# A two-block attention and feed-forward kernel: the start, the row maxima, the gated unit and the drawn order are changed

## The chip, the cores and the metric

The kernel runs on one core of one Trainium2 chip. The metric is the device time of one execution in microseconds (us); the median of three runs is 1132.83.

## The reference

The input x has 128 sequences of 64 tokens with 128 features (8192 tokens), and so has a context c. Four blocks follow each other, each with a residual addition:

```python
x = x + L0_xattn(layernorm(x), ctx)   # normalises again, 16 heads of 8, sigmoid gate, normalises its output
x = x + L0_ffn(layernorm(x))          # silu(x W1) * (x W2), two 512x512 layers with gelu, 512 to 128
x = x + L1_xattn(layernorm(x), ctx)   # 16 heads of 8, softmax, output projection
x = x + L1_ffn(layernorm(x))          # relu(x W1 + b1) W2 + b2
```

Everything is in 32-bit floats. The softmax subtracts a maximum per row before the exponential.

## The kernel before

The 8192 tokens are cut into 17 chunks: the first and the last have two groups of 128 tokens, the other fifteen have four. Each chunk passes through the four blocks (`attention0`, `ffn0`, `attention1`, `ffn1`). Each block is written as a Python generator that yields one operation (`Op`) at a time with the engine, a name, the buffers that it takes (`get`) and gives back (`put`). A planner (`Order`) runs on the host while the program is built. At each step it takes, among the operations that are next in their streams, the one that can start first by a table of durations (`LENGTHS`), and issues its instructions. So the order on every engine is fixed by the planner. It keeps a clock for each engine. Where two operations could start at the same time, priority decides, plus a small pseudo-random number (`draw`) whose seed comes from the list `DRAWS`, one entry for each 50 us of the planner's TensorE clock; a seed of 0 means that nothing is added.

```python
seed = DRAWS[min(int(self.clock[PE] / STRETCH), len(DRAWS) - 1)]
...
key = (t + (0.6 if other else 0.0), prio + s.op.draw, n)
```

TensorE (PE) writes to eight banks of PSUM. A score tile takes four banks of one half at once; all else takes one. In the first 95 us of the planner's clock, `fill` puts matmuls of zeros into gaps that the planner sees on PE:

```python
n = int((t - self.clock[PE]) * 0.8 / FILLER)   # FILLER is 0.11
```

Before that, `busy(60, 7)` issues sixty such matmuls (L428) by hand at the very start. Their operand is filled by GpSimd (POOL), and nothing reads what they write.

The loads go out from SyncE's queue at the start, in an order written by hand: the first chunk's context and input, the small constants, the first attention's weights (`wa`), the second chunk, and then the larger weights and the third chunk. `landed` holds when the planner takes each of them to be there; its clock begins with the first landing, which is about 3 us after the start of the trace.

The start of a chunk runs through these lines. VectorE (DVE) takes the moments (L541, L543), POOL makes a reciprocal square root (L526 to L559), ScalarE (ACT) or DVE normalises (L568, L572), PE transposes (L582), ACT or DVE scales and copies (L589, L591), and PE multiplies for keys (L618), queries (L606) and values (L631). ACT or DVE writes masked copies of keys and queries (L597, L599), for which the masks (L479 to L487) must be there.

Attention works on half a chunk at a time (`attend`): scores (L658, packed in rows of the array), the row maxima from PSUM (L662, DVE), the maxima as three bf16 parts (L672 to L675, DVE or POOL), their transposition (L679) and copy (L682, ACT), the scores once more with the maxima taken off (L691, with the selection matrix `asel`), the exponential (L696, ACT), the weighted values (L710, packed in columns, with the value buffer `vblk`), masking (L720 to L724), reciprocal (L727, L728) and the product on POOL (L742). The operation for the maxima takes one of four buffers `nm` and gives back all four banks when it is over.

The value buffers `vblk` (three) and the buffers `nm` (four) are filled with constants by POOL at the start (`blanks`: L493, L496, L498), each as soon as POOL is free for it. The additions of a row vector to x (L848, L1070, L1092) are POOL's too, and so are the sums of weights that the multiplication scheme of the two 512x512 layers needs (L896).

The gated unit (`gated`, four times a chunk) takes two banks at once, issues both products (L903, L904), then tanh (L907, ACT) and two fused operations on DVE (L909, L910) as one operation. Its result goes into the two square layers (`square`): differences on POOL (L938), products (L956), sums (L982) and gelu (L975).

Of the kernel before, what the change touches and what calls it, by code (L numbers as in the profile page):

```python
# [18 lines left out]
SEQ = 64  # L19
# [7 lines left out]
HS = 4  # L27
# [11 lines left out]
for _n, _w in _COLS:  # L39
# [10 lines left out]
N_VB, N_NM = 3, 4  # L50
# [11 lines left out]


STRETCH = 50.0
DRAWS = [97, 0, 427, 0, 249, 0, 0, 0, 575, 0, 0, 112, 0, 817, 0, 39, 412, 0, 615, 329, 0, 15, 762, 0]
SPREAD = 0.1
SWAP = [*range(16, 32), *range(16)]

# [2 lines left out]
PE, DVE, ACT, POOL, SP = "PE", "DVE", "ACT", "POOL", "SP"  # L71
NONE = ""
# [4 lines left out]
    PE: {  # L77
        "bias": (0.22, 0.25), "transpose": (0.46, 0.15), "q": (0.86, -0.2), "k": (0.94, -0.2), "v": (0.89, 0.15),
        "scores": (0.99, 0.2), "max transpose": (0.07, 0.2), "scores less max": (1.17, 0.2),
        "weighted values": (0.92, 0.2), "tokens": (0.22, 0.15), "tokens 4": (0.9, 0.15), "w12": (1.73, -0.2),  # L80
        "product": (0.865, -0.2), "f1": (0.865, -0.2),
    },
    DVE: {
        "bias+": 0.28, "masks": 1.2, "gate weights": 0.4, "folds": 1.9, "moments": 1.07, "z": 1.3, "copied": 0.68,
        "scaled": 0.75, "qx": 1.5, "kx": 1.5, "vb": 1.8, "max": 2.3, "parts": 0.8, "reciprocal": 2.2, "o2": 0.83,
        "from bank": 0.68, "gate sums": 1.3, "gate": 0.4, "gained": 1.1, "gated": 1.45, "sum": 0.68, "saved": 0.68,
        "relu": 0.7,
    },
    ACT: {
# [233 lines left out]
def kernel(  # L323
# [16 lines left out]
    nc = tc.nc  # L340
# [65 lines left out]
    order = Order(RESOURCES)  # L406
# [3 lines left out]
    hm = load("hm", [P, 2, 2, 2], headmask.rearrange("p (n s t) -> p n s t", n=2, s=2))  # L410
# [15 lines left out]
    def busy(n, bank):  # L426
        for _ in range(n):
            nc.tensor.matmul(banks[:, bank, 0:P], blank, blank, start=True, stop=True)  # L428

    order.busy = busy  # L430
    busy(60, 7)
    ident = const.tile([P, P], F32, tag="ident", name="ident")
    make_identity(nc, ident)

    mask = const.tile([P, 4], F32, tag="mask", name="mask")
    half_mask = const.tile([P, 2, 4], F32, tag="half_mask", name="half_mask")
# [39 lines left out]

    def masks():
        yield Op(DVE, "masks")
        nc.vector.tensor_tensor(half_mask[:, 0, 0:2], hm[:, 0, 0, :], hm[:, 0, 1, :], ALU.add)  # L479
        nc.vector.tensor_tensor(half_mask[:, 1, 0:2], hm[:, 1, 0, :], hm[:, 1, 1, :], ALU.add)  # L480
        nc.vector.tensor_tensor(half_mask[:, 0, 2:4], hm[:, 0, :, 0], hm[:, 0, :, 1], ALU.add)
        nc.vector.tensor_tensor(half_mask[:, 1, 2:4], hm[:, 1, :, 0], hm[:, 1, :, 1], ALU.add)
        nc.vector.tensor_tensor(mask, half_mask[:, 0, :], half_mask[:, 1, :], ALU.add)
        for t, i, name in (
            (bk0, 2, "L0_xattn_bk"), (bq0, 0, "L0_xattn_bq"), (bk1, 2, "L1_xattn_b_k"), (bq1, 0, "L1_xattn_b_q"),
        ):
            nc.vector.tensor_scalar(t, mask[:, i : i + 2], colv(name), None, ALU.mult)  # L487

    def blanks():

        for i in range(N_NM):
            yield Op(POOL, "blank", put=[("nm", i)])
            nc.gpsimd.memset(nmax[i], 0.0)  # L493
            if i < N_VB:
                yield Op(POOL, "blank values", put=[("vb", i)])
                nc.gpsimd.memset(vblk[i], 0.0)  # L496
                for par in range(2):
                    nc.gpsimd.memset(vblk[i][64 * par : 64 * par + 64, :, 1, par, :], 1.0)  # L498
# [4 lines left out]
    fold = const.tile([P, 2, 32], F32, tag="fold", name="fold")  # L503
# [139 lines left out]
    def attend(got, half, halves):  # L643
# [11 lines left out]
        for s in range(HS):  # L655
            for g in range(4):
                h = slice(32 * g, 32 * g + 32)
                nc.tensor.matmul(sc[:, g, s, :], qs[h, s, :], ks[h, s, :], start=True, stop=True)  # L658
        mx = yield Op(DVE, "max", get={"nm": 1}, put=pe.slots["sc"])
        nm = nmax[mx.slots["nm"][0][1]]  # L660
        m = small.tile([P, 4, 2 * HS], F32, tag="m", name="m")
        nc.vector.tensor_reduce(  # L662
            m,
            sc.rearrange("p g s (j k) -> p g (s j) k", j=2),
            AX.X,
            ALU.max,
            negate=True,
        )
# [125 lines left out]
    def folds():  # L794

        yield Op(DVE, "folds")

        nc.vector.tensor_copy(identb, ident)
        nc.vector.tensor_tensor(
            fold, ident[:, 0:64].rearrange("p (r c) -> p r c", r=2), ident[:, 64:128].rearrange("p (r c) -> p r c", r=2), ALU.add  # L800
        )
        nc.vector.tensor_tensor(fold[:, 0, :], fold[:, 0, :], fold[:, 1, :], ALU.add)
        for j in range(1, 3):
            nc.vector.tensor_tensor(
                fold[:, 0, 0:8], fold[:, 0, 0:8], fold[:, 0, 8 * j : 8 * j + 8], ALU.add
            )
        for s in range(HS):
            nc.vector.tensor_copy(
                asel[:, s, :].rearrange("p (j k) -> p j k", j=2),
                fold[:, 0, 2 * s : 2 * s + 2].unsqueeze(2).to_broadcast([P, 2, 64]),  # L810
            )
# [86 lines left out]
        made_weights[l] = [a[0][0], a[0][1], s[2], a[1][1], s[0], s[1], a[1][0]]  # L898

    def gated(k, zT, n, free, d):  # L900
        pe = yield Op(PE, "w12", get={"bank": 2, "wk": 1}, put=free)
        pa, pb = (tile_of(s, (P, n)) for s in pe.slots["bank"])
        nc.tensor.matmul(pa, w12[:, 0, k * P : (k + 1) * P], zT, start=True, stop=True)  # L903
        nc.tensor.matmul(pb, w12[:, 1, k * P : (k + 1) * P], zT, start=True, stop=True)  # L904
        yield Op(ACT, "tanh", prio=-1)
        th = tile_of(pe.slots["wk"][0], (P, n))
        nc.scalar.activation(th, pa, AF.Tanh, scale=half_s1[:, k : k + 1])  # L907
        yield Op(DVE, "gated", put=pe.slots["bank"] + pe.slots["wk"], prio=-1)
        nc.vector.scalar_tensor_tensor(th, th, 1.0, pa, ALU.add, ALU.mult)  # L909
        nc.vector.scalar_tensor_tensor(  # L910
            d[k // 2][0][:, :, k % 2, :],
            th.rearrange("p (t c) -> p t c", t=2),
            half_s12[:, k : k + 1],
            pb.rearrange("p (t c) -> p t c", t=2),
            ALU.mult,
            ALU.mult,
        )
# [97 lines left out]
    def ffn0(ci, prio):  # L1015
        xt, ng = x_sb[ci], GROUPS[ci]
        z, fz = yield from normalised(xt, ng)
        zT, fz = yield from transposed(z, ng, fz)
        fz = Last(fz, 4)
        b, made = {}, []  # L1020
        n = ng * P
        yield from two_halves(b, n)
# [174 lines left out]
```

## Time and profile before

| | us |
|---|---|
| median of three runs (lowest, highest) | 1132.83 (1132.09, 1133.68) |
| the profiled execution, whole | 1132.17 |
| its span, first to last instruction | 1130.3 |
| PE busy | 1100.1 |
| DVE busy | 866.8 |
| ACT busy | 726.0 |
| POOL busy | 504.9 |

The profile is of one execution. A row of a group gives the line, the engine, the operation, what is written and read, how often, the busy time and the mean duration of one. PE's busy time counts matmuls whose ends are modelled; PEld is the loading of weights, which overlaps them. The granted clock is the share of its full clock that PE was given.

### The profile page before, as it was taken

What the parts mean: (1) busy time and instruction counts of PE and PEld (TensorE: products, weight loads), DVE (VectorE), ACT (ScalarE), POOL (GpSimd) and SP (SyncE); (2) the same over time, 40 slices, a digit from 0 to 9 for tenths busy, and PEclk for the clock granted to TensorE, in tenths of its full rate; (3) what the DMA queues carried; (4) which work ended last, traced back from release to release, by engine and by line L of the source; (5) the groups of instructions that cost most, each with busy time, mean ns of one, the idle gap of its engine ahead of it and who ended that gap; (6) DMA issues with size and microseconds to landing.
All of it is one profiled execution on the core that took longest, in us unless ns stands there. A gap on an engine that the chain in (4) does not pass through costs nothing.

```text
span 1130.3 us, 32935 instructions
## 1 busy us (share of the span) xinstructions
PE 1100.1 (97%) x13871; PEld 868.5 (77%) x13871; DVE 866.8 (77%) x2139; ACT 726.0 (64%) x1279; POOL 504.9 (45%) x882
## 2 busy tenths in 40 slices
PE   7699999999999999999999999999999999999998
PEld 6577687778876778878676887777778887789786
DVE  7887969889877777567978687788789888643773
ACT  5467767666775776576646686667867675545553
POOL 6745545445534445333326355335345546352221
PEclk9999999999999999999999999999999999999999
DMA  7001000000001001001100000000000000000001
GB/s 244 12 2 29 21 11 21 11 1 20 12 2 34 2 2 39 1 3 38 49 20 20 11 21 11 12 19 12 11 11 12 11 7 11 1 1 1 12 20 43
DMA packets 35444, 23.23 MB, mean 21 GB/s; under 512 B 1504, under 2 KB 34272, under 8 KB 35168
## 3 DMA queue, kind: packets, MB, share of 16 engines
q1 hardware_dynamic: 35296, 21.13, 6.3%
q8 instruction: 109, 1.79, 0.7%
q14 instruction: 39, 0.32, 0.1%
HBM read 16.93 MB, written 4.19 MB: 19 GB/s over the span
## 4 chain that ended last, share of the span: by engine, by line
PE 87%; DVE 9%; ACT 2%; issue 1%; POOL 1%; DVEq 0%; ACTq 0%; POOLq 0%
PE banks L956 33%; PE banks L770 12%; PE banks L691 7%; PE banks L710 5%; PE banks L658 5%; PE banks L1080 5%; PE banks L903 4%; PE banks L904 4%; PE banks L582 4%; DVE m L662 3%; PE banks L631 3%; PE banks L618 2%; PE banks L606 2%; DVE su L727 1%; PE banks L428 1%
## 5 line engine op out<-in xcount | busy, mean ns | idle before, releaser
L662 DVE TENSOR_REDUCE m<-banks 128x32 f32<-128x2048 f32 x64 | 145.9, 2281 | 17.6 <-PE banks L658 16.9
L742 POOL TENSOR_TENSOR wk<-av,rec 128x256 f32<-128x256 f32 x64 | 46.9, 733 | 220.6 <-DVE rec L728 198.0
L696 ACT ACTIVATE e<-banks 128x2048 f32<-128x2048 f32 x64 | 120.2, 1877 | 36.3 <-PE banks L691 29.1
L956 PE MATMUL banks<-hd,wh 128*128 128x256 f32 (+1 forms) x544 | 127.7, 371 | 0.4 <-DVE wk L909 0.4
L956 PE MATMUL banks<-wk,wh 128*128 128x256 f32 (+1 forms) x544 | 127.5, 371 | 0.0
L956 PE MATMUL banks<-wk,ws 128*128 128x256 f32 (+1 forms) x544 | 126.3, 371 | 0.8 <-POOL wk L938 0.7
L727 DVE RECIPROCAL su<-su 128x256 f32<-128x256 f32 x64 | 111.5, 1742 | 0.0
L956 PEld LDWEIGHTS banks<-wk,wh 128*128 128x128 f32 x544 | 96.4, 190 | 18.0 <-issue 5.7
L975 ACT ACTIVATE hd<-hd,col 128x256 f32<-128x256 f32 (+1 forms) x204 | 88.8, 488 | 31.7 <-DVE hd L982 30.9
L956 PEld LDWEIGHTS banks<-hd,wh 128*128 128x128 f32 x544 | 95.4, 190 | 16.4 <-issue 4.1
L956 PEld LDWEIGHTS banks<-wk,ws 128*128 128x128 f32 x544 | 94.7, 190 | 16.5 <-issue 3.3
L982 DVE TENSOR_TENSOR hd<-banks,hd 128x512 f32<-128x512 f32 (+1 forms) x102 | 66.7, 656 | 52.9 <-PE banks L956 45.3
L529 POOL TENSOR_TENSOR nr<-nv,neg_half 128x4 f32<-128x4 f32 (+1 forms) x102 | 99.7, 978 | 8.5
L938 POOL TENSOR_TENSOR wk<-hd,wk 128x512 f32<-128x512 f32 (+1 forms) x68 | 82.4, 1212 | 40.4 <-DVE hd L910 29.0
L512 ACT COPY hd<-banks 128x512 f32<-128x512 f32 (+1 forms) x68 | 37.9, 557 | 73.0 <-PE banks L956 67.9
L568 ACT ACTIVATE wk<-x,nb,nr 128x128 f32<-128x128 f32 x192 | 79.0, 484 | 7.1 <-POOL nb L559 6.8
L658 PEld LDWEIGHTS banks<-kx,qx 32*128 32x128 f32 x2048 | 62.8, 186 | 22.4 <-issue 10.0
L710 PEld LDWEIGHTS banks<-e,vblk 128*32 128x32 f32 x4096 | 60.2, 110 | 24.0 <-issue 7.6
L658 PE MATMUL banks<-kx,qx 32*128 32x128 f32 x2048 | 74.6, 282 | 2.5 <-ACT qx L597 1.2
L710 PE MATMUL banks<-e,vblk 128*32 128x64 f32 x4096 | 70.4, 220 | 2.2 <-ACT e L696 2.2
L691 PE MATMUL banks<-qx,kx 32*128 32x128 f32 x2048 | 71.7, 277 | 0.0
L909 DVE SCALAR_TENSOR_TENSOR wk<-wk,banks 128x512 f32<-128x512 f32 (+1 forms) x68 | 43.9, 646 | 33.1 <-ACT wk L907 33.0
(136 smaller groups left out, 2399.2 us busy)
## 6 DMA issues: line engine op xcount, KB each, us to landing
c<-in_c_dram SPq DMA_DIRECT2D x30, 256.0 KB, 3.0
x<-in_x_dram SPq DMA_DIRECT2D x15, 256.0 KB, 3.6
out_dram<-x SPq DMA_DIRECT2D x15, 256.0 KB, 2.3
wh<-in_w_h_dram SPq DMA_DIRECT2D x1, 2048.0 KB, 12.4
c<-in_c_dram SPq DMA_DIRECT2D x4, 128.0 KB, 2.7
wa<-in_w_a_dram SPq DMA_DIRECT2D x2, 256.0 KB, 5.1
w<-in_w_dram SPq DMA_DIRECT2D x1, 512.0 KB, 7.9
wf<-in_w_f_dram SPq DMA_DIRECT2D x2, 256.0 KB, 6.7
```

Of the source, the lines that this page charges most:

```text
L529: nc.gpsimd.tensor_tensor(rs, ve, neg_half[:, 0:ng], ALU.pow)
L568: nc.scalar.activation(z[:, g, :], src[:, g, :], AF.Identity, bias=nb[:, g : g + 1], scale=rs[:, g : g + 1])
L658: nc.tensor.matmul(sc[:, g, s, :], qs[h, s, :], ks[h, s, :], start=True, stop=True)
L662: nc.vector.tensor_reduce(m, sc.rearrange("p g s (j k) -> p g (s j) k", j=2), AX.X, ALU.max, negate=True,)
L691: nc.tensor.matmul(sT[:, g, s, :], lhs, rhs, start=(n == 0 and s == 0), stop=(n == 1), skip_group_check=True)
L696: nc.scalar.activation(e.rearrange("p g s i q -> p (g s i q)"), sT.rearrange("p g s c -> p (g s c)"), AF.Exp, scale=SCALE,)
L710: nc.tensor.matmul(po[32 * g : 32 * g + 32, i, s, :], vb[:, 4 * (half * HS + s) + g, i : i + 2].rearrange("p h j d -> p (h j d)"), e[:, g, ...
L727: nc.vector.reciprocal(su, su)
L770: nc.tensor.matmul(ps[:, g, :], lhs(g), w, start=(n == 0), stop=(n == len(blocks) - 1),)
L938: nc.gpsimd.tensor_tensor(T[m][0], x(), y(), ALU.subtract)
L956: nc.tensor.matmul(pieces[bank][0][:, o], w[:, k, o * P : (o + 1) * P], x[:, k], start=(new and k == 0 and o == 0), stop=(k == 1), skip_gr ...
L975: nc.scalar.activation(out(i, t)[:, o], (src or out(i, t))[:, o], AF.Gelu, scale=colv(scale, 2 * i + o))
```

## The change

Six things are changed. Forty zero-matmuls are issued at the start instead of sixty, and the planner's PE clock is set to 2.5 us behind them. The masks are made by two reductions over two axes instead of five additions, and the fold and the selection matrix by one reduction and one copy instead of four additions and four copies. The third value buffer's fill, and the fourth small one behind it, wait until the planner's clock has passed the landing of the first square layer's weights (24 us). The row maxima are taken in two operations of two banks each; the first gives back two banks, and only the second takes the buffer `nm`. The gated unit's second product is a stream of its own with priority 2, taking its own bank; the fused DVE operations become two planner operations. The durations in the planner's table follow these, and `DRAWS` is a new list without zeros.

```diff
-DRAWS = [97, 0, 427, 0, 249, 0, 0, 0, 575, 0, 0, 112, 0, 817, 0, 39, 412, 0, 615, 329, 0, 15, 762, 0]
+DRAWS = [71454, 18189, 18189, 18189, 18189, 68446, 18189, 18189, 18189, 18189, 35898, 18189, 18189, 18189, 23663, 18189, 18189, 18189, 39503, 18189, 49075, 18189, 62786, 18189]
...
-    busy(60, 7)
+    busy(40, 7)
+    order.clock[PE] = 2.5
...
-        nc.vector.tensor_tensor(half_mask[:, 0, 0:2], hm[:, 0, 0, :], hm[:, 0, 1, :], ALU.add)
-        nc.vector.tensor_tensor(half_mask[:, 1, 0:2], hm[:, 1, 0, :], hm[:, 1, 1, :], ALU.add)
-        nc.vector.tensor_tensor(half_mask[:, 0, 2:4], hm[:, 0, :, 0], hm[:, 0, :, 1], ALU.add)
-        nc.vector.tensor_tensor(half_mask[:, 1, 2:4], hm[:, 1, :, 0], hm[:, 1, :, 1], ALU.add)
-        nc.vector.tensor_tensor(mask, half_mask[:, 0, :], half_mask[:, 1, :], ALU.add)
+        for i, order_of in ((0, "p n s t -> p t n s"), (2, "p n s t -> p s n t")):
+            nc.vector.tensor_reduce(mask[:, i : i + 2], hm.rearrange(order_of), AX.XY, ALU.add)
...
             if i < N_VB:
+                if i == N_VB - 1:
+                    yield Op(NONE, "free", after=landed[7])
                 yield Op(POOL, "blank values", put=[("vb", i)])
...
-        mx = yield Op(DVE, "max", get={"nm": 1}, put=pe.slots["sc"])
+        m = small.tile([P, 4, 2 * HS], F32, tag="m", name="m")
+        for two in range(2):
+            gs = slice(2 * two, 2 * two + 2)
+            mx = yield Op(DVE, "max", get={} if two == 0 else {"nm": 1}, put=sorted(pe.slots["sc"], key=lambda x: x[1])[gs])
+            nc.vector.tensor_reduce(
+                m[:, gs],
+                sc[:, gs].rearrange("p g s (j k) -> p g (s j) k", j=2),
+                AX.X,
+                ALU.max,
+                negate=True,
+            )
...
-        nc.vector.tensor_tensor(
-            fold, ident[:, 0:64].rearrange("p (r c) -> p r c", r=2), ident[:, 64:128].rearrange("p (r c) -> p r c", r=2), ALU.add
+        rows_of_8 = ident.rearrange("p (r j c) -> p c r j", j=4, c=8)[:, :, :, 0:3]
+        nc.vector.tensor_reduce(fold, rows_of_8, AX.XY, ALU.add)
+        nc.vector.tensor_copy(
+            asel.rearrange("p s (j k) -> p (s j) k", j=2), fold.unsqueeze(2).to_broadcast([P, 2 * HS, SEQ])
         )
...
     def gated(k, zT, n, free, d):
-        pe = yield Op(PE, "w12", get={"bank": 2, "wk": 1}, put=free)
+        got = {}
+
+        def other():
+            pe = yield Op(PE, "w12", get={"bank": 1}, put=free)
+            got["pb"] = (tile_of(pe.slots["bank"][0], (P, n)), pe.slots["bank"])
+            nc.tensor.matmul(got["pb"][0], w12[:, 1, k * P : (k + 1) * P], zT, start=True, stop=True)
+
+        pe = yield Op(PE, "w12", get={"bank": 1, "wk": 1}, put=free)
...
-        nc.tensor.matmul(pb, w12[:, 1, k * P : (k + 1) * P], zT, start=True, stop=True)
         yield Op(ACT, "tanh", prio=-1)
...
+        second = yield (other(), 2)
+        yield Op(DVE, "gated a", put=pe.slots["bank"], prio=-1)
         nc.vector.scalar_tensor_tensor(th, th, 1.0, pa, ALU.add, ALU.mult)
+        yield [second]
+        yield Op(DVE, "gated b", put=got["pb"][1] + pe.slots["wk"], prio=-1)
```

More of the change, by code (lines that the diff above doesn't have):

```diff
@@ L79 @@
         "scores": (0.99, 0.2), "max transpose": (0.07, 0.2), "scores less max": (1.17, 0.2),
-        "weighted values": (0.92, 0.2), "tokens": (0.22, 0.15), "tokens 4": (0.9, 0.15), "w12": (1.73, -0.2),
+        "weighted values": (0.92, 0.2), "tokens": (0.22, 0.15), "tokens 4": (0.9, 0.15), "w12": (0.865, -0.2),
         "product": (0.865, -0.2), "f1": (0.865, -0.2),
@@ L83 @@
     DVE: {
-        "bias+": 0.28, "masks": 1.2, "gate weights": 0.4, "folds": 1.9, "moments": 1.07, "z": 1.3, "copied": 0.68,
-        "scaled": 0.75, "qx": 1.5, "kx": 1.5, "vb": 1.8, "max": 2.3, "parts": 0.8, "reciprocal": 2.2, "o2": 0.83,
-        "from bank": 0.68, "gate sums": 1.3, "gate": 0.4, "gained": 1.1, "gated": 1.45, "sum": 0.68, "saved": 0.68,
+        "bias+": 0.28, "masks": 0.9, "gate weights": 0.4, "folds": 1.3, "moments": 1.07, "z": 1.3, "copied": 0.68,
+        "scaled": 0.75, "qx": 1.5, "kx": 1.5, "vb": 1.8, "max": 1.19, "parts": 0.8, "reciprocal": 2.2, "o2": 0.83,
+        "from bank": 0.68, "gate sums": 1.3, "gate": 0.4, "gained": 1.1, "gated a": 0.68, "gated b": 0.75, "sum": 0.68, "saved": 0.68,
         "relu": 0.7,
@@ L435 @@
     mask = const.tile([P, 4], F32, tag="mask", name="mask")
-    half_mask = const.tile([P, 2, 4], F32, tag="half_mask", name="half_mask")
     im, pm = (lambda i: mask[:, i : i + 1]), (lambda i: mask[:, 2 + i : 3 + i])
@@ L502 @@
     identb = const.tile([P, P], BF16, tag="identb", name="identb")
-    fold = const.tile([P, 2, 32], F32, tag="fold", name="fold")
+    fold = const.tile([P, 2 * HS], F32, tag="fold", name="fold")
     asel = const.tile([P, HS, P], BF16, tag="asel", name="asel")
@@ L658, in attend @@
                 nc.tensor.matmul(sc[:, g, s, :], qs[h, s, :], ks[h, s, :], start=True, stop=True)
-        mx = yield Op(DVE, "max", get={"nm": 1}, put=pe.slots["sc"])
-        nm = nmax[mx.slots["nm"][0][1]]
[L661 to L668, printed above, removed]
+        m = small.tile([P, 4, 2 * HS], F32, tag="m", name="m")
[9 more added lines that the diff above has]
+            )
+        nm = nmax[mx.slots["nm"][0][1]]
         op = yield Op((DVE, POOL), "parts")
@@ L798, in folds @@
         nc.vector.tensor_copy(identb, ident)
-        nc.vector.tensor_tensor(
-            fold, ident[:, 0:64].rearrange("p (r c) -> p r c", r=2), ident[:, 64:128].rearrange("p (r c) -> p r c", r=2), ALU.add
-        )
[L802 to L811, printed above, removed]
+        rows_of_8 = ident.rearrange("p (r j c) -> p c r j", j=4, c=8)[:, :, :, 0:3]
+        nc.vector.tensor_reduce(fold, rows_of_8, AX.XY, ALU.add)
+        nc.vector.tensor_copy(
+            asel.rearrange("p s (j k) -> p (s j) k", j=2), fold.unsqueeze(2).to_broadcast([P, 2 * HS, SEQ])
+        )
         nc.vector.tensor_scalar(half_s1, col[:, COL["L0_ffn_w1_s"]], 0.5, None, ALU.mult)
@@ L900, in gated @@
     def gated(k, zT, n, free, d):
-        pe = yield Op(PE, "w12", get={"bank": 2, "wk": 1}, put=free)
-        pa, pb = (tile_of(s, (P, n)) for s in pe.slots["bank"])
+        got = {}
[4 more added lines that the diff above has]
+        pe = yield Op(PE, "w12", get={"bank": 1, "wk": 1}, put=free)
+        pa = tile_of(pe.slots["bank"][0], (P, n))
         nc.tensor.matmul(pa, w12[:, 0, k * P : (k + 1) * P], zT, start=True, stop=True)
-        nc.tensor.matmul(pb, w12[:, 1, k * P : (k + 1) * P], zT, start=True, stop=True)
         yield Op(ACT, "tanh", prio=-1)
@@ L907, in gated @@
         nc.scalar.activation(th, pa, AF.Tanh, scale=half_s1[:, k : k + 1])
-        yield Op(DVE, "gated", put=pe.slots["bank"] + pe.slots["wk"], prio=-1)
+        second = yield (other(), 2)
+        yield Op(DVE, "gated a", put=pe.slots["bank"], prio=-1)
         nc.vector.scalar_tensor_tensor(th, th, 1.0, pa, ALU.add, ALU.mult)
+        yield [second]
+        yield Op(DVE, "gated b", put=got["pb"][1] + pe.slots["wk"], prio=-1)
+        pb = got["pb"][0]
         nc.vector.scalar_tensor_tensor(
@@ L1018, in ffn0 @@
         zT, fz = yield from transposed(z, ng, fz)
-        fz = Last(fz, 4)
+        fz = Last(fz, 8)
         b, made = {}, []
```

## The prediction

> **What bounds the kernel now.** I read the page's busy shares first, then the busy time by stretches, then the waits of TensorE (PE), then the timeline of the first 20 us.
>
> ```profile
> span 1130.3 us, 32935 instructions
> PE 1100.1 (97%) x13871; PEld 868.5 (77%) x13871; DVE 866.8 (77%) x2139; ACT 726.0 (64%) x1279; POOL 504.9 (45%) x882
> ...
> PE 87%; DVE 9%; ACT 2%; issue 1%; POOL 1%; DVEq 0%; ACTq 0%; POOLq 0%
> ```
>
> PE is the bound and 87% of the chain. What an edit can win is PE's time that does no needed work: waits, zero-matmuls, and stretches at a low clock. The next table shows where it is (columns: stretch, its length, busy us and count of PE, PEld, DVE, ACT, POOL, then granted clock, DMA share, GB/s).
>
> ```profile
> 0.00:20.00 20.00, 16.34 (x178) 13.99 (x179) 14.38 (x64) 10.64 (x23) 15.18 (x39) 1.00 0.84 282
> 20.00:40.00 20.00, 14.30 (x458) 12.48 (x458) 16.79 (x46) 10.76 (x18) 10.06 (x20) 1.00 0.25 65
> 40.00:60.00 20.00, 14.95 (x152) 11.25 (x152) 16.73 (x43) 8.33 (x16) 14.82 (x30) 0.85 0.05 14
> 60.00:80.00 20.00, 18.65 (x328) 15.93 (x325) 15.81 (x54) 13.48 (x27) 7.57 (x14) 0.98 0.01 2
> 80.00:100.00 20.00, 20.00 (x146) 15.31 (x145) 16.45 (x49) 14.64 (x31) 12.59 (x20) 1.00 0.10 28
> ```
>
> PE idles 4 to 6 us of every 20 until 60 us, and its clock there falls to 0.85 on average: two stretches of 3.41 us (43.8 and 57.4 us) at half. From 80 us it is full. To price this I gave each matmul the smallest spacing that the trace shows for its shape (429 ns for 512 columns, 215.5 for 256, 111 for 128; a packed group of scores 1103 ns). Needed work then is 1041.5 us, and 84.2 us are something else: 34.8 before 64 us, 3.4 in 64 to 80, 46.0 after. Of those 46.0, some 17 are the 176 entries into a packed group (row or column tiles of the array), 98 ns each at the median; another 17 are waits over 120 ns, less that entry; the rest are joints of a few ns. So the steady part has about 17 us that a better order could win. Whom PE waited for, over all:
>
> ```profile
> PE banks L679 <- DVE nmax L675: 4.9, 5, 1.4
> PE banks L770 <- DVE m L662: 2.7, 1, 2.7
> PE banks L710 <- ACT e L696: 2.2, 2, 1.1
> PE banks L770 <- ACT e L696: 2.1, 1, 2.1
> PE banks L582 <- DVE m L662: 1.6, 1, 1.6
> ...
> PE banks L679 <- POOL nmax L675: 1.3, 2, 1.0
> ...
> PE banks L691 <- DVE m L662: 0.7, 2, 0.5
> ```
>
> (Columns: total us, times, longest.) With one of 0.2 us for L658, 11.4 us in 12 waits stand behind the row maxima (L662) or their three-part copy (L675).
>
> **The head.** The timeline shows PE and ACT:
>
> ```profile
> 7.22 0.44 PE L790 MATMUL banks<-gw,ones 128*128 128x129 f32 x2
> 7.50 1.73 PE L428 MATMUL banks<-blank 128*128 128x128 bf16 x28
> 9.06 0.39 PE L582 MATMUL banks<-ident,wk 128*128 128x128 f32 x2
> ...
> 5.57 0.88 ACT L568 ACTIVATE wk<-c,nb,nr 128x128 f32<-128x128 f32 x2 [1.22 <-POOL nb L559]
> 9.49 0.56 ACT L589 ACTIVATE wk<-banks,col 128x256 f32<-128x256 f32 x1 [3.04 <-PE banks L582]
> ```
>
> The first transposes (L582) have their input at 6.45 us (5.57 + 0.88) and start at 9.06, since 95 zero-matmuls (60 by hand, 7 and 28 by the planner's `fill`) lie ahead. ACT idles 3.04 us for them. The changed kernel has 40 by hand: at the 107 ns that the trace shows between cold ones they end at 0.98 + 4.28 = 5.26. The planner is also told that PE is taken until 2.5 on its own clock. Before, it gave 28 for a gap of 28 x 0.11 / 0.8 = 3.85; starting from 2.5 + 0.22 (one bias product) instead of about 1.2, the gap is 2.35 and the fill 17. So 5.26, then two passes of L790 (about 0.3), then 17 zero-matmuls, the first few cold: 1.2 to 1.5. L582 starts at about 7.0. **Gain 2.0 us.** What is late next: L618 needs the weights wa, issued at 2.70 with 2.9 to 7.2 us to landing for the two such loads, so at worst 9.9 against today's 10.10. Bounds: -2.6 (transposes at once at 6.45) and -0.2; I take the middle value, as 2.70 + 5.1 (median) = 7.8 lies before L618's new time of 8.1. These 2 us carry to the end only if DVE, 84% busy in 20 to 60 us, moves along; it waits for the same chain (L591, L599, L662), so I let it.
>
> Does the lower count leave the clock cold? In this trace spacing falls from 107 to 56 ns at 6.2 us, 5.2 us after the first zero-matmul. The Trainium skill, "TensorE: Matmul & The Clock Gate" (Part 1), speaks against the change: the full clock needs one wholly busy window of about 3.4 us, and windows run free of the program. Forty last 4.28 us, which by that rule can miss a whole window; then the clock would rise up to 3.4 us later, and the real passes before it (L582, L618, L631, some 1.5 us at full clock) would take twice as long: +1.5. By the row, with 17 planner zero-matmuls behind the forty, PE stays busy to 7 us and the rise stays near 6.2: 0. I take 0 and keep +1.5 for the range.
>
> **Constants by sums.** In the masks five adds (153 to 175 ns each, 0.57 from 6.53 to 7.10) become two reductions; the nearest row is an 8-element add at 166, so 0.3 to 0.4: -0.2. In the folds 0.88 us of adds (4.82 to 5.70) become one reduction of 96 elements (nearest: the 64-wide add, 217), and four copies to asel (0.63 in all) one of 512 elements (nearest: 0.66, a 128x512 copy): -0.6. That is 0.8 us of DVE ahead of the second chunk's moments at 7.67. What hides it: DVE next idles 0.54 us for x from DMA at 9.35 and 0.34 for PE at 10.84. Sum 0; bounds -0.8 and +0.3 (strided reading of ident, unseen here).
>
> **A fill later.** The third value buffer's fill (1.38 + 0.65 us, from 15.62) and the fourth small one behind it move past 24 us of the planner's clock, some 27 us of the trace. Today they hold back POOL's L848 to 17.79 to 19.08, where it stands beside DVE's L673: that took 1.14 us against a mean of 0.275. L673 lies on the chain max, parts, L679 (19.72), exp. With L848 two us earlier it is clear of it: **-0.9**. The fill then goes into POOL's time beside the weights L896 (first one 27.30; their result is needed at 61.7), with DVE's L599 unharmed beside such a fill (0.99 at 13.09 as at 10.84). If that buffer or the fourth maximum tile is wanted before 29 us, PE waits up to 2: bounds -0.9 and +1.1. No DMA is moved or added; SP's queue keeps its order, apart from what the new order makes of buffers coming free.
>
> **Maxima in halves.** One reduction of 2048 columns (2281 ns, 64 times) becomes two of 1024. From 128x128 at 279 and 128x512 at 690 ns (both PSUM sources) a fixed part of 142 follows; half then is 142 + 1069 = 1211, a pair +141. Back to back it is less: the four 222 ns copies of L808 stood in 0.63 us, so 64 of each fixed part is hidden, and a pair costs +77. DVE: +5 to +9 us, 77.4% at most, no bound. On the path: the 12 waits above, 12 x 0.077 = **+0.9**. In return two of four banks come free 1.2 us earlier. L770 and L582 each waited for one bank behind L662: 2 x -1.2 = **-2.4**; L691 and L658 need all four and gain nothing. Another DVE operation can also go between the halves.
>
> **Gated unit apart.** PE passes (L903, L904) and DVE instructions (L909, L910) stay the same in number. The second product's stream begins once tanh is planned, so it takes its bank some 0.7 us later (L907: 659 ns), beside L909 (646 ns), which frees the first bank; L910 then follows the product (2 x 429 ns) by little more than today. What waits: L910 now may stand behind other DVE work; POOL's L938 waits for it (56.7 us of POOL waiting on L910 already), and PE's L956 waited only 0.7 us for L938. That slack covers it: 0. If gone: 68 x up to 0.7 us, though only on a few of them. zT is held for eight releases, four as before plus four products already queued: 0.
>
> **The order drawn anew.** Every tie on every engine falls differently. The unit of cost is known, the sign not: the remaining 12 us of steady waits, entries at 98 ns (353 tiling changes now; twenty fewer would be -1), and two half-clock stretches at up to 1.7 us each. I take **-1.6**, about a seventh of those 12, because finer pieces leave fewer forced waits; bounds -9 and +8.
>
> Sum: -2.0 - 0.9 + 0.9 - 2.4 - 1.6 = **-6.0**. The profiled execution took 1132.17 (span 1130.3, 1.87 around it), so 1126.2; the median of the runs is 0.66 higher: **1126.8**.
>
> **Rivals.** (1) Only the head: 1130.8. The new order re-rolls 17 us of waits without winning any, and `fill` puts back zero-matmuls. For it: 97% leaves little, and DVE at 84% in 20 to 60 us may keep its own pace. Against: two one-bank waits behind L662. Chance 0.20. (2) Slower: the halved maxima. Each pair is 141 ns longer, with other work between; if each of 64 is exposed, +9.0, less 2.0 of the head: 1139.8. It decides once over 2.0/64 = 31 ns of each is exposed. Against: only 12 maxima are waited for now. Chance 0.12. (3) More: both half-clock stretches go (-3.4), half the steady waits (-8), head and fill -2.9: 1118.5. Chance 0.13. The forecast itself has 0.55, with a range of its own of 1122 to 1130.5.
>
> **Numbers.** Within 0.2% (2.3 us, about what a measurement of this kernel can tell from no change) reaches from 1130.6 to 1135.1. Rival 1 lies at its edge: two fifths faster. So faster 0.55 + 0.13 + 0.07 = 0.75, same 0.13, slower 0.12. The range 1116.5 to 1134 holds the forecast, rivals 1 and most of 3, and leaves out rival 2.
>
> **What would show it.** L582 first at about 7.0 us, 60 or so zero-matmuls before it; L673 near 0.27; L662 x128 at about 1.2 us; no L770 or L582 wait behind L662; PE's busy time some 5 us less. Wrong if PE waits behind L662 and L675 pass 20 us, if spacing stays at 107 ns past 8 us, or if time before 64 us grows.

## The result, and the profile after

| | before | after |
|---|---|---|
| median of the runs, us (number) | 1132.46 (4) | 1142.03 (4) |
| lowest, highest | 1129.65, 1133.68 | 1139.13, 1143.72 |
| the profiled execution: whole, span | 1132.17, 1130.3 | 1139.13, 1137.1 |

The change made the kernel slower. The ratio is 1.009, with a 95% interval of 1.0074 to 1.0107. The forecast was 1126.8 with a range up to 1134, so it was wrong in sign and in range. The profiled execution of the changed kernel is the fastest of its four: the two profiles below lie 7.0 us apart, the medians 9.6.

In the changed file the lines move: transposes L581, scores L657, maxima L662, three-part copy L673 to L676, its transposition L680, scores less maxima L692, exponential L697, weighted values L711, second products L903, fused operations L909 and L913, differences L941, products L959, row vector's addition L841.

The page's busy times, the sum of the chain, and PE's waits (total us, times, longest) of the changed kernel:

```profile
span 1137.1 us, 32939 instructions
PE 1105.6 (97%) x13857; PEld 866.3 (76%) x13857; DVE 888.6 (78%) x2261; ACT 734.8 (65%) x1272; POOL 492.6 (43%) x834
...
PE 85%; DVE 11%; ACT 1%; issue 1%; DMA 0%; SPq 0%; POOL 0%; DVEq 0%; ACTq 0%; POOLq 0%
```

```profile
PE banks L680 <- DVE nmax L676: 5.4, 7, 1.5
PE banks L711 <- ACT e L697: 3.8, 3, 2.1
PE banks L581 <- ACT wk L567: 2.9, 3, 1.4
PE banks L711 <- DVE gate L835: 1.5, 1, 1.5
PE banks L959 <- DVE m L662: 1.4, 1, 1.4
PE banks L657 <- DVE av L725: 1.0, 1, 1.0
PE banks L959 <- POOL wk L941: 1.0, 1, 1.0
```

DVE is busy 21.8 us longer and takes 11% of the chain instead of 9%. POOL is busy 12.3 us less. No single wait stands out. The two one-bank waits of before (L770 and L582 behind L662) are gone, as forecast; others have come: L959 behind L662 and L711 behind the gate are new, and L711 and L581 behind ACT have grown (from 2.2 and 1.4).

Where the time went shows when PE's spacing is priced as in the prediction. Needed work is 1041.5 us in both kernels. What is not needed work was 84.2 us before and is 90.6 now:

| stretch, us | before | after |
|---|---|---|
| 0 to 64 | 34.8 | 35.5 |
| 64 to 80 | 3.4 | 3.7 |
| 80 to 200 | 6.1 | 10.7 |
| 200 to 800 | 30.3 | 27.7 |
| 800 to the end | 9.6 | 13.1 |

The stretches are cut at equal times. Needed work done by 20 us is 7.3 us against 6.1 before: the changed kernel is 1.2 us ahead. By 40 us both have done 16.8; by 64 us the changed one is 0.9 behind (27.5 against 28.4), by 80 us 0.3 (40.5 against 40.8), by 200 us 5.5 (149.3 against 154.8). So the head's gain is real but gone by 40 us, and most of the loss falls in 80 to 200 us. The windows (length, busy us and count of PE, PEld, DVE, ACT, POOL, granted clock, DMA share, GB/s) read, first the kernel before in 80 to 200 us, then the changed one:

```profile
80.00:200.00 120.00, 118.13 (x1487) 93.57 (x1485) 99.37 (x252) 84.08 (x154) 60.82 (x110) 1.00 0.07 19
```

```profile
0.00:20.00 20.00, 15.27 (x181) 12.57 (x185) 15.49 (x61) 11.12 (x23) 16.42 (x40) 1.00 0.80 280
20.00:40.00 20.00, 14.46 (x438) 12.65 (x435) 17.96 (x52) 9.84 (x15) 6.81 (x11) 0.91 0.24 66
40.00:60.00 20.00, 16.11 (x134) 11.98 (x134) 18.33 (x56) 9.83 (x21) 14.05 (x25) 0.96 0.05 15
...
120.00:140.00 20.00, 17.46 (x282) 13.79 (x281) 19.84 (x54) 13.16 (x22) 13.88 (x27) 1.00 0.01 3
...
80.00:200.00 120.00, 114.64 (x1428) 87.16 (x1430) 109.01 (x267) 76.92 (x132) 51.10 (x87) 1.00 0.06 17
```

In 80 to 200 us DVE is busy 9.6 us longer while ACT is busy 7.2 and POOL 9.7 us less; between 120 and 140 us DVE is busy 19.84 of 20 us and PE idles 2.5. The clock is full in both. The new order laid work on DVE, the busiest of the three engines beside PE there. Three parts of it can be counted in the trace. All 18 copies into the value buffers in this stretch run on DVE and none on ACT (8 and 9 before), about 4.2 us; over the whole kernel 80 of 136 are DVE's, against 64. The four instructions of L674 take 2.7 us together and the four of L676 as much, where the two of each line took 0.4 before: they are held up, as is shown below. The maxima add 1.0.

### The profile page after: what moved, and what is told of

Same layout as the page of the kernel before. It is cut to its first block, busy times and chain, and to the rows that moved or that the text cites. A ratio compares the mean times of both kernels' runs of the same rounds, so it can differ in the third digit from the quotient of the medians.

```text
span 1137.1 us, 32939 instructions
## 1 busy us (share of the span) xinstructions
PE 1105.6 (97%) x13857; PEld 866.3 (76%) x13857; DVE 888.6 (78%) x2261; ACT 734.8 (65%) x1272; POOL 492.6 (43%) x834
## 4 chain that ended last, share of the span: by engine, by line
PE 85%; DVE 11%; ACT 1%; issue 1%; DMA 0%; SPq 0%; POOL 0%; DVEq 0%; ACTq 0%; POOLq 0%
PE banks L959 32%; PE banks L771 12%; PE banks L692 6%; PE banks L657 5%; PE banks L711 5%; PE banks L899 5%; PE banks L903 5%; PE banks L1083 5%; PE banks L581 3%; PE banks L617 2%; PE banks L630 2%; PE banks L605 2%; DVE m L662 2%; DVE su L728 1%; DVE x L869 1%
## 5 line engine op out<-in xcount | busy, mean ns | idle before, releaser
L662 DVE TENSOR_REDUCE m<-banks 128x16 f32<-128x1024 f32 x128 | 152.0, 1214 | 22.1 <-PE banks L657 21.9
L697 ACT ACTIVATE e<-banks 128x2048 f32<-128x2048 f32 x64 | 120.2, 1878 | 23.5 <-PE banks L692 21.8
L959 PE MATMUL banks<-hd,wh 128*128 128x256 f32 (+1 forms) x544 | 128.1, 372 | 1.4 <-DVE m L662 1.4
L959 PE MATMUL banks<-wk,wh 128*128 128x256 f32 (+1 forms) x544 | 127.6, 370 | 0.0
L959 PE MATMUL banks<-wk,ws 128*128 128x256 f32 (+1 forms) x544 | 124.2, 371 | 1.5 <-POOL wk L941 1.0
L959 PEld LDWEIGHTS banks<-hd,wh 128*128 128x128 f32 x544 | 95.4, 190 | 22.9 <-issue 7.7
L511 ACT COPY hd<-banks 128x512 f32<-128x512 f32 (+1 forms) x74 | 41.4, 559 | 109.8 <-PE banks L959 108.7
L959 PEld LDWEIGHTS banks<-wk,wh 128*128 128x128 f32 x544 | 96.3, 190 | 17.1 <-issue 5.5
L959 PEld LDWEIGHTS banks<-wk,ws 128*128 128x128 f32 x544 | 95.2, 190 | 17.9 <-issue 3.9
L941 POOL TENSOR_TENSOR wk<-hd,wk 128x512 f32<-128x512 f32 (+1 forms) x68 | 82.1, 1209 | 18.2 <-PE banks L605 6.7
L567 ACT ACTIVATE wk<-x,nb,nr 128x128 f32<-128x128 f32 x192 | 78.8, 485 | 12.1 <-POOL nb L558 11.6
L657 PEld LDWEIGHTS banks<-kx,qx 32*128 32x128 f32 x2048 | 65.1, 190 | 24.7 <-issue 10.6
L711 PEld LDWEIGHTS banks<-e,vblk 128*32 128x32 f32 x4096 | 60.3, 110 | 25.2 <-issue 8.7
L657 PE MATMUL banks<-kx,qx 32*128 32x128 f32 x2048 | 77.3, 287 | 2.0 <-DVE av L725 1.0
L711 PE MATMUL banks<-e,vblk 128*32 128x64 f32 x4096 | 70.5, 221 | 5.6 <-ACT e L697 3.8
L692 PE MATMUL banks<-qx,kx 32*128 32x128 f32 x2048 | 71.6, 277 | 0.0
L941 POOL TENSOR_TENSOR wk<-hd 128x512 f32<-128x512 f32 (+1 forms) x34 | 41.1, 1210 | 63.9 <-DVE hd L913 45.7
```

Source lines behind the costliest of these rows:

```text
L567: nc.scalar.activation(z[:, g, :], src[:, g, :], AF.Identity, bias=nb[:, g : g + 1], scale=rs[:, g : g + 1])
L662: nc.vector.tensor_reduce(m[:, gs], sc[:, gs].rearrange("p g s (j k) -> p g (s j) k", j=2), AX.X, ALU.max, negate=True,)
L692: nc.tensor.matmul(sT[:, g, s, :], lhs, rhs, start=(n == 0 and s == 0), stop=(n == 1), skip_group_check=True)
L697: nc.scalar.activation(e.rearrange("p g s i q -> p (g s i q)"), sT.rearrange("p g s c -> p (g s c)"), AF.Exp, scale=SCALE,)
L711: nc.tensor.matmul(po[32 * g : 32 * g + 32, i, s, :], vb[:, 4 * (half * HS + s) + g, i : i + 2].rearrange("p h j d -> p (h j d)"), e[:, g, ...
L941: nc.gpsimd.tensor_tensor(T[m][0], x(), y(), ALU.subtract)
```

## The experiments

Each time is the median of the runs; each ratio is to the kernel before, run on the same chip, with its 95% interval. "The plan" in the expectations is the end of the order on the planner's own clock, by its table of durations. The plans of all these kernels lie within one per cent of each other, from 1107.8 to 1117.7 us. That of the kernel before is 1117.7 and that of the changed one 1115.0: the planner took the change for 2.7 us of gain.

**Is it one of the parts, in the order as it is?** Four kernels keep an order and change one thing. The first takes the whole maximum at the place of the first half (the second half's place stays empty):

```diff
-            nc.vector.tensor_reduce(
...
+            if two == 0:
+                nc.vector.tensor_reduce(m, sc.rearrange("p g s (j k) -> p g (s j) k", j=2), AX.X, ALU.max, negate=True)
```

> The changed kernel with its order untouched: at the place of the first half the whole maximum over four banks is taken in one instruction, and nothing is issued at the place of the second; the planner plans as if nothing had happened. DVE loses 64 fixed parts (1.214 x 2 - 2.28 = 0.15 us each, 9.5 us busy), and no DVE work can slip between the halves. Theory A (the halves' price on DVE is the loss, rival 2 of the prediction): 64 x 0.15 come back, 1142 falls to 1133 to 1135. Theory B (the drawn order is the loss, whatever the parts): 1139 to 1143, within 2 us of the changed kernel. Theory C (half-clock stretches at the start): unchanged, 1139 to 1143.

1155.3, 1.0203 [1.0189, 1.0217], outside all three expectations. In this order, which was planned for halves, whole maxima cost 13 us more, so taking the halves away wins nothing back: this speaks against rival 2. How much of the 13 is the empty place was not separated; the granted clock was 0.990 to 0.993 against 0.994 to 0.997.

```diff
-        n = int((t - self.clock[PE]) * 0.8 / FILLER)
+        n = int((t - self.clock[PE]) * 1.3 / FILLER)
```

> The changed kernel with its order untouched, but the planner's fill in the first 95 us of its clock is 1.3/0.8 times as many zero-matmuls in each gap, so that PE idles less there. Theory C (the runs at 1141 to 1144 have more half-clock stretches than the profiled one at 1139, 1.7 us each, and this is the loss): no half-clock stretch between 20 and 64 us, 1134 to 1137, and less scatter. Theories A and B: within 2 us of the changed kernel, 1140 to 1144, as zero-matmuls may also stand in the way.

1143.64, 1.0099 [1.0084, 1.0113]. More zero-matmuls moved the second half-clock stretch from 58 to 65 us and won nothing; the median execution had a granted clock of 0.998. It is not the clock.

```diff
-    busy(40, 7)
+    busy(60, 7)
```

> The changed kernel with its order untouched and sixty zero-matmuls by hand instead of forty. The prediction's head term says that this gives back about 20 x 0.056 to 0.107 us: +1 to +2 (1142 to 1144). Theory B says the same or nothing (the first chunks wait for loads and for DVE anyway): 0 to +1. If the lower count had left the clock cold (theory C): -1 to -3, 1139 to 1141.

1143.4, 1.0099 [1.0083, 1.0114], against 1.009 [1.0074, 1.0107] with forty: by the ratios the twenty zero-matmuls are worth 1.0 us, and the intervals are too wide to tell that from nothing or from the forecast 2.0.

The fourth goes the other way: the order of before with forty zero-matmuls, the constants by sums, and the two half maxima one behind the other:

```diff
-    busy(60, 7)
+    busy(40, 7)
...
+        for gs in (slice(0, 2), slice(2, 4)):
+            nc.vector.tensor_reduce(m[:, gs], sc[:, gs].rearrange("p g s (j k) -> p g (s j) k", j=2), AX.X, ALU.max, negate=True)
```

> The kernel before with its own order and draws, the planner's table untouched, and only what needs no new order: forty zero-matmuls instead of sixty, the constants by sums over two axes, and each maximum as two halves back to back. By the prediction's terms: head -1 to -2, constants 0, halves +0.9: 1131 to 1132.5. Theory A: halves cost up to 64 x 0.15 = 9.5, so 1138 to 1141. Theory B: within 2 us of before, 1130.5 to 1134.

1131.29, 0.9999 [0.9989, 1.0008]. Three of the six edits together are neutral in the old order (-1.2 to +0.9 us; the forecast's terms for them sum to -1.1). The loss lies in what else comes with the change: the order, the buffers' fill, and the gated unit.

**A structure, or a list of draws?** Every structure was run with two further lists for `DRAWS`; nothing else differs between the two kernels of a pair. The second list of the structure before stands here for all:

```diff
-DRAWS = [97, 0, 427, 0, 249, 0, 0, 0, 575, 0, 0, 112, 0, 817, 0, 39, 412, 0, 615, 329, 0, 15, 762, 0]
+DRAWS = [73386, 73084, 96466, 96466, 7445, 96466, 96466, 73132, 96466, 96466, 96466, 96466, 96466, 5660, 96466, 96466, 96466, 96568, 96466, 96466, 96466, 96466, 96466, 96466]
```

> The kernel before with nothing changed but DRAWS: a list found by a search over the planner alone (some 600 lists, its own last clock as the measure), whose planned end is as early as that of the changed kernel. Theory B1 (orders of the same planned length scatter on the chip by several us, and the list of before is a lucky one): 1134 to 1144, slower than before. Theory B2 (the plan is good for this structure, and the changed structure is what the plan misjudges): 1127 to 1131, as much faster as planned.

> As the run before it, with another list from another search, planned some 0.2% earlier still. B1: anywhere in 1132 to 1144 and not in line with the plan. B2: 1125 to 1129, faster than the run before it.

1130.61 and 1127.09: both fast, as B2 has it.

> The changed kernel with nothing changed but DRAWS: a list from the same kind of search, planned within 0.1% of its own. B1: between 1130 and 1144, with the same mean as the two lists on the kernel before. B2 (structure): 1138 to 1144 again.

> As the run before it, with a list that the plan takes to be 0.6% shorter than its own. B1: 1128 to 1140. B2: at least 10 over the plan's gain, 1133 to 1138, and slower than the best list on the kernel before. If the plan holds differences between lists, it is the faster of the two on this structure.

1139.48 and 1128.79: far apart, as B1 has it.

Then the changed kernel with the maximum whole again (one operation, 2.3 in the planner's table), and with the gated unit whole again:

```diff
-        for two in range(2):
...
+        mx = yield Op(DVE, "max", get={"nm": 1}, put=pe.slots["sc"])
```

> The changed kernel with the row maxima whole again, in the planner too (one operation of 2.3, as before), everything else as changed, and a list of draws from a search over the planner, planned some 0.1% shorter than the changed kernel's. So far the chip took 1.3 to 1.5% over the plan on the structure before (three lists) and 1.8 to 2.4% on the changed one (three lists). Theory M (the halved maxima are what the plan misjudges): it falls back to 1.3 to 1.5% over the plan, 1128 to 1131. Theory G (the gated unit apart is): 1134 to 1141, as slow as the changed structure.

> As the run before it with a second list of the same planned length: the same numbers, M 1128 to 1131, G 1134 to 1141; the distance between the two tells what a list does at one planned length.

1140.15 and 1130.82.

```diff
-        pe = yield Op(PE, "w12", get={"bank": 1, "wk": 1}, put=free)
+        pe = yield Op(PE, "w12", get={"bank": 2, "wk": 1}, put=free)
...
-        yield Op(DVE, "gated a", put=pe.slots["bank"], prio=-1)
+        yield Op(DVE, "gated", put=pe.slots["bank"] + pe.slots["wk"], prio=-1)
```

> The changed kernel with the gated unit whole again (both banks at once, both products in one operation, both DVE steps in one), everything else as changed, the maxima in halves, and a list of its own of the same planned length. Theory G: back to 1.3 to 1.5% over the plan, 1128 to 1130. Theory M: 1134 to 1140.

> As the run before it with a second list, planned 0.2% longer: G 1130 to 1133, M 1136 to 1143.

1131.37 and 1144.0. Each structure came out once fast and once slow, so neither M nor G holds.

| structure | its own list | list 1 | list 2 |
|---|---|---|---|
| before | 1 | 0.9987 [0.9979, 0.9994] | 0.9959 [0.9944, 0.9973] |
| after | 1.009 [1.0074, 1.0107] | 1.0067 [1.0047, 1.0087] | 0.9969 [0.9957, 0.998] |
| after, maximum whole | | 1.0073 [1.0056, 1.009] | 0.9991 [0.9983, 0.9998] |
| after, gated unit whole | | 1.0001 [0.9992, 1.001] | 1.0102 [1.0078, 1.0126] |

With only the draws changed, the changed kernel goes from 1142.03 to 1128.79 us, faster than before. Each of the three new structures has a list near 1.00 and one near 1.01; neither halves nor a second product apart decides. Within a structure the list does, by some 10 us. That the new list has no zeros is not the reason: lists 1 and 2 of the structure before have none either. The plan tells only a part: list 2 of the changed structure has a plan 5.5 us shorter than list 1, about half of the 10.7 us that it is faster; but the two lists with the whole maximum have plans equal to within a thousandth (1113.7 and 1113.3), and are 9.3 us apart. (The slow list of the last row ran at a clock of 0.988 to 0.993, with six half-clock stretches in its profile before the last 2 us; of its 12 us over the kernel before that is a part.)

A last one of this kind has both whole and a list with a shorter plan:

> The changed kernel with both the maxima and the gated unit whole again, so that only forty zero-matmuls with the planner's clock set, the constants by sums and the later fill stay, and a list of draws from a search over the planner, planned 0.6% shorter than the changed kernel's own. If what stays is what the plan misjudges: 2% over the plan, 1130 to 1133. If not (S or L): 1.3 to 1.6% over the plan as on the kernel before, 1122 to 1126, faster than both kernels.

1137.34, 1.0053 [1.0035, 1.0071], at a clock of 0.988 to 0.992. The shortest plan of all (1107.8) did not give a fast kernel; it took 2.7% over the plan, outside both expectations. Over their plans the three lists of the structure before took 1.3 to 1.5%, the eight of the new structures 1.6 to 2.7%. So one rival stays open: what all new structures share (the planner's clock set behind forty zero-matmuls, the constants, the later fill) may make slow orders more frequent. Three lists on the old structure are too few to exclude it, and no run took these parts away in a newly drawn order.

The fast list of the changed structure in the stretch where the slow one lost most:

```profile
80.00:200.00 120.00, 119.02 (x1555) 92.49 (x1554) 103.00 (x267) 84.06 (x145) 56.45 (x103) 1.00 0.05 15
```

DVE has as many instructions as with the slow list (267) in 6 us less, ACT has 7.1 us more, and PE idles 1.0 us instead of 5.4. Of the 17 copies into the value buffers here 9 run on DVE and 8 on ACT, and no DVE instruction is held up in the way shown next; with the slow list 11 are, for 8.8 us.

**Are held-up instructions what makes an order slow?** In the trace of after, around 725 us, DVE (first fence) and POOL (second; start, duration, engine, line, what) read:

```profile
724.77 1.20 DVE L674 TENSOR_TENSOR m<-m,nmax 128x32 f32<-128x32 f32 x1
726.00 1.17 DVE L675 CAST nmax<-m 128x32 bf16<-128x32 f32 x1
727.21 0.19 DVE L676 TENSOR_TENSOR nmax<-m,nmax 128x32 bf16<-128x32 f32 x1
```

```profile
724.65 1.27 POOL L841 TENSOR_TENSOR x<-x,row 128x512 f32<-128x512 f32 x1
725.88 1.27 POOL L941 TENSOR_TENSOR wk<-hd,wk 128x512 f32<-128x512 f32 x1
```

L674 starts after L841 of POOL and ends with it (725.97 and 725.92); L675 starts after L941 and ends with it (727.17 and 727.15). Alone, each takes 0.2 us. PE waits right behind:

```profile
727.46 0.23 PE L680 MATMUL banks<-identb,nmax 128*128 128x128 bf16 x1 [1.46 <-DVE nmax L676]
```

Counting all DVE instructions that last over 0.4 us longer than the 10% level of their kind: 36 before (30.0 us in excess of that level), 42 after (35.3 us). Each of them ends 0.02 to 0.16 us after a POOL tensor_tensor of 128x512 or 128x256 that ran beside it. In the three-part copy, which PE waits for, it is 7 instructions of 96 before (7.0 us) and 15 of 144 after (13.3 us); the new order puts 36 of the 64 copies on DVE instead of 24. The Trainium skill, "SBUF — State Buffer" (Who interferes with whom), has the rule: a DVE instruction with two inputs in SBUF contends with a POOL instruction that reads SBUF, and so does one in a mode that uses two ports, which a copy or cast can enter; whichever issues first has the shared pair of ports for its whole run, and the other is blocked. The trace agrees for each of the 36 and 42; by it the 1.2 us is the remaining run of POOL's tensor_tensor, not DVE's own work.

The planner, in both kernels, has a rule against just this:

```python
PORT = {"z", "parts", "gate sums", "gained"}   # DVE operations; every POOL operation counts too
...
            if op.port:
                t = max(t, self.port[DVE if e == POOL else POOL])
```

On its own clock no such DVE operation (93 before, 105 after) overlaps one of POOL's. At the place above the copy is planned for 710.8 to 711.6 and L841 for 712.9. On the chip the copy came 13.7 us later than planned and L841 11.7 (some 3 us of both is where the clocks begin), so they met. All 42 instructions, and all but one of the 36, belong to these four kinds of operation: they are places where the times of the table had drifted from those of the chip.

Nor do the hold-ups alone tell a slow order from a fast one. Counted in the same way, the fast list of the changed structure (1128.79) has 39 (33.1 us), and 15 of them (13.8 us) in the three-part copy, as many as the slow one; only their places differ, and PE waits half as long behind them:

```profile
PE banks L680 <- DVE nmax L676: 2.7, 5, 0.9
```

Over the eleven orders run here the excess is 25 to 41 us in the six of 1127 to 1133 us and 35 to 48 in the five of 1137 to 1144: related, but overlapping.

Three kernels take a part of the hold-up away with the order untouched: the copy on POOL always; POOL's additions and differences in two halves each, so that a hold-up is half as long; and both.

```diff
-        by = nc.gpsimd if op.engine == POOL else nc.vector
+        by = nc.gpsimd
```

> The changed kernel with its order untouched, but the three-part copy of the maxima (L673 to L676) is always issued on POOL, where the planner had put 36 of 64 on DVE. In the changed kernel's profile 15 of the 144 such DVE instructions take about 1.1 us instead of 0.2 (13.1 us in all), each beside a 1.2 us POOL tensor_tensor, and the longest PE waits (160.5, 725.9) stand right behind them. Theory S (DVE's small SBUF operations are held up by a running POOL instruction, which the drawn order runs into more often): 4 to 8 us come back, 1134 to 1138. Theory L (only how the order falls, no one mechanism): within 3 of 1142, or slower, since POOL's queue gets 36 operations of 0.95 us that it was not planned for.

```diff
+    def pool_halves(out, x, y, f):
+        n = out.shape[1] // 2
+        for i in range(2):
+            h = slice(i * n, i * n + n)
+            nc.gpsimd.tensor_tensor(out[:, h], x[:, h], y[:, h], f)
...
-        nc.gpsimd.tensor_tensor(xt, xt, rowv("L0_xattn_ln_o_b", ng), ALU.add)
+        pool_halves(xt, xt, rowv("L0_xattn_ln_o_b", ng), ALU.add)
...
```

> The changed kernel with its order untouched; POOL's operations of 512 columns (1.21 us: differences L941, additions to x, sums of weights) are issued as two of 256 (0.73 us each). Theory S: what holds DVE up ends at the end of the running POOL instruction, so its excess (37 us of DVE time over the normal lengths) falls by a third or more and 2 to 4 us come back, 1138 to 1140. Theory L: POOL is 0.25 us later at some 170 places, 1142 to 1146.

> The changed kernel, order untouched, with both edits: the three-part copy always on POOL, and POOL's 512-column operations as two of 256. Each alone took about 0.3% off. Theory S with the two adding up (what is left for the second are the normalising operations L563, L829, L869 and L571, 24 us of excess): 1134 to 1137. If both only remove the same waits behind the copies: 1137 to 1139, as each alone.

And the two controls, the same edits on the kernel before:

> The control for the first edit: the kernel before, order untouched, the three-part copy always on POOL. There 7 of 96 such DVE instructions are held up (6.9 us) against 15 of 144 (13.1 us). Theory S: a smaller gain than on the changed kernel, 0 to -2, 1130 to 1132. If the copy on POOL is simply better anywhere: -3 or more, below 1129.

> The same edit on the kernel before, order untouched, as the control: its DVE excess is 31.8 us, 7 stretched parts (6.9 us). Theory S: 0 to -2, 1130 to 1132. Theory L: 0 to +3.

| edit | on after | gain | excess, us | on before | gain | excess, us |
|---|---|---|---|---|---|---|
| none | 1.009 [1.0074, 1.0107] | | 35.3 | 1 | | 30.0 |
| copy on POOL | 1.0063 [1.0046, 1.008] | 0.0027 | 22.6 | 0.997 [0.996, 0.998] | 0.0030 | 24.4 |
| POOL in halves | 1.0064 [1.0046, 1.0082] | 0.0026 | 30.0 | 0.9996 [0.9985, 1.0007] | 0.0004 | 30.1 |
| both | 1.0016 [1.0009, 1.0023] | 0.0074 | 18.3 | not run | | |

The excess is that of the count above. The halves took less off it than expected, and nothing on the kernel before. The copy on POOL made the kernel before faster than theory S has it (1128.25): it is better there too.

The same place with the copy on POOL, and PE's wait behind it over the whole kernel:

```profile
721.40 0.29 POOL L674 TENSOR_TENSOR m<-m,nmax 128x32 f32<-128x32 f32 x1
721.75 0.21 POOL L675 CAST nmax<-m 128x32 bf16<-128x32 f32 x1
722.04 0.38 POOL L676 TENSOR_TENSOR nmax<-m,nmax 128x32 bf16<-128x32 f32 x1
722.48 0.23 PE L680 MATMUL banks<-identb,nmax 128*128 128x128 bf16 x1
```

```profile
PE banks L680 <- POOL nmax L676: 1.2, 3, 0.8
```

The 1.46 us wait is gone, and of 5.4 us behind DVE's copy 1.2 behind POOL's are left (in the fastest of its four executions, 1134.0; the others took 1138.4 to 1139.5). So the hold-up is real and costs time: with half of the excess gone 7.4 parts in 1000 come back. But the controls limit what it explains. The copy's hold-up costs the kernel before as much (0.0030), so it does not tell the two apart. What differs is POOL in halves (0.0026 against 0.0004), by less than the intervals can tell, and perhaps what both do together. If the two controls add up, before would stand at 0.9966 with both edits and after at 1.0016: 0.0050 of the 0.0090 remain, and the hold-up would explain some 0.4 of the 0.9%. On the changed kernel the two edits gave more together than their sum (0.0074 against 0.0053), so it may be less; this estimate rests on a sum that was not run. DVE's total load is not the bound either: the first edit takes 37.1 us off DVE (888.6 to 851.5) for 3 us of time.

What stays open is the rest, at least half. The trace shows it as waits of PE behind late work on DVE, ACT and POOL, above all in 80 to 200 us where DVE is busy 91% of the time and makes all value copies, and again after 800 us (+3.5 us, not traced to a cause). That moving the value copies to ACT would win it back was not run.

## Why the prediction was wrong, point by point

- **The order drawn anew, -1.6 with bounds -9 and +8: the step that failed.** What is left for it is about +9: the result was +9.6, and the head, the constants and the halves issued back to back come to nothing in the old order (0.9999). The gated unit and the later fill are in this remainder; no run separates them from a new order. The text called the sign unknown and then took a negative value, "because finer pieces leave fewer forced waits". The runs show no such rule: with the same pieces, three lists gave 1.009, 1.0067 and 0.9969, a scatter of 13 us. The bounds were near right and should have set the range; 1134 was only 7 above the forecast, where the +8 of this term alone asked for 1136.
- **The head, -2.0: near in place, for another reason, and wrong in worth.** L581 starts at 7.36 us (7.0 forecast), with 58 zero-matmuls ahead (57), and the first scores come at 13.07 instead of 14.13. That 7.36 is near 7.0 is luck. The zero-matmuls were over at 5.95, and PE then waited 1.41 us for ACT, which got its input later than the 6.45 taken over from the trace of before: the new order gave POOL and ACT x before c, so that ACT began its two L567 at 6.82, where the first had begun with c at 5.57:

```profile
0.98 3.69 PE L428 MATMUL banks<-blank 128*128 128x128 bf16 x40 [0.98 <-POOL blank L424]
4.51 0.44 PE L791 MATMUL banks<-gw,ones 128*128 128x129 f32 x2
4.78 1.17 PE L428 MATMUL banks<-blank 128*128 128x128 bf16 x18
7.36 0.71 PE L581 MATMUL banks<-ident,wk 128*128 128x128 f32 x2 [1.41 <-ACT wk L567]
...
6.82 0.88 ACT L567 ACTIVATE wk<-x,nb,nr 128x128 f32<-128x128 f32 x2 [1.81 <-POOL nb L558]
```

  The lead of 1.2 us at 20 us is gone by 40. "So I let it" was the weak sentence: DVE is busy 17.96 of 20 us in 20 to 40 and 18.33 in 40 to 60. That DVE sets the pace there is argued from these shares; no run shows it.
- **A fill later, -0.9: the local effect right, its reading too narrow.** In that copy L673 and L674 take 0.18 and 0.19 us (the second of them, L673 before, took 1.14). But the 1.14 us was one of 36 such places, and a new order moves them about; the prediction priced one and did not ask for the others.
- **The halves: sized right on DVE.** L662 takes 1214 ns (1211 forecast), and DVE's maxima grow by 6.1 us (5 to 9 forecast); the +0.9 on the path was not measured alone:

```profile
L662 DVE TENSOR_REDUCE m<-banks 128x16 f32<-128x1024 f32 x128 | 152.0, 1214 | 22.1 <-PE banks L657 21.9
```

- **One-bank waits, -2.4: gone as forecast, and replaced.** The passes at L771 and L581 no longer wait behind L662; L959 does (1.4 us).
- **Constants and gated unit, 0.** The constants fit: 0.9999 with them. For the gated unit alone nothing was measured apart from lists; its structures overlap.
- **Rivals.** The slower rival's number, 1139.8, was near the result and its mechanism is not what the runs show: whole maxima in the same order were slower, and halves back to back in the old order cost nothing. No rival had the order itself turning out badly, though the term had a bound of +8.
- **The signs to watch missed.** Two of the three signs of error did not come true (waits behind maxima and copies far under 20 us, full clock at 3.7 us), and the third hardly (time before 64 us that is not needed work grew from 34.8 to 35.5), while PE's busy time rose by 5.5 us instead of falling by 5. They watched the parts, not the order.
- **The pricing of PE.** The spacings called the smallest are the usual ones for 128 columns and for a packed group of scores (the smallest are 109 and 995 ns). Both kernels are priced alike, so the comparison stands.

## What to carry to other kernels

When a change redraws the order of a packed kernel, its price is the scatter between orders, here 9 us between two lists that the planner takes for equal, and it outweighs the parts: hold the order fixed to judge a part, and draw several orders for each structure to judge a structure. A planner with fixed durations can keep apart what holds each other up on its own clock alone: once the chip's times drift by a microsecond, they meet. Here small DVE copies on the path did better on POOL in both orders tried; that one edit made the kernel before 0.3% faster (1128.25), and other lists gave 1127.09 for the old structure and 1128.79 for the new one, all better than both kernels compared here. An earlier start on the bounding engine is worth only what the other engines let through: 1.2 us at 20 us were gone by 40.

## What the hardware did that I had not expected

- A running POOL tensor_tensor holds a DVE instruction on SBUF until it ends: 1.2 us for a copy of 0.2 us, 36 and 42 times in the two kernels. With POOL's operations in halves, the changed kernel's 42 hold-ups of over 0.4 us (0.84 us on average) became 63 of 0.48 us.
- Zero-matmuls reached full clock at 3.7 us in the changed kernel and at 6.2 us in the one before, though both begin at 0.98 us. The number issued cannot be the reason, as at 3.7 us the forty were still running. In the traces of all twenty kernels here, every change of the granted clock lies a whole number of 3.413 us after the first (31.01, 34.43, 58.32 and 61.73 are 8, 9, 16 and 17 such steps after 3.71), and where this grid falls differs from one execution to the next. The first rise, at 3.66 to 7.00 us, came at the first grid point before which PE had been busy for enough of a step: 78% of the step, counted from the first zero-matmul, was enough (whole maximum, list 2; 80% in the changed kernel), 76% was not (more filler; sixty by hand), nor 54% in the kernel before. So a wholly busy window, on which the prediction's +1.5 rests, was not needed.
- The half-clock stretches are 3.41 us long in both, at 43.8 and 57.4 before, at 31.0 and 58.3 after; sixty per cent more filler (0.8 to 1.3) only moved the second.
